# A graph layer's edge network: first layer as eight 32-row products, placed later in the step, and ten more one-hot picks

## The chip, the cores and the metric

The kernel runs on one core of one Trainium2 chip. The metric is the device time of one execution in microseconds; the median of 14 runs of the kernel before is 2398.38 us (2378.84 to 2437.09). A core has a matrix engine (TensorE, in the profile PE for its products and PEld for its weight loads), a vector engine (VectorE, DVE), a scalar engine (ScalarE, ACT), GpSimd (POOL) and a queue engine (SyncE, SP). Products land in PSUM, which has eight banks of 512 fp32 columns in each of 128 partitions.

## The reference, cut to what matters

N = 6250 nodes with F = 64 features, E = 200000 edges sorted by their target node, D = 32 edge attributes, M = 9 edge components, H = 64 hidden units.

```
w     = silu(edge_attr_32 @ W1 + b1) @ W2 + b2          # E x 9: 32 -> 64 -> 9, for every edge
h_src = x[src]                                          # E x 64: a gather of rows
msg   = einsum('ef,em,fmg->eg', h_src, edge_attr_9 * w, W_tp)
agg   = segment_sum(msg, dst, N) / 4
gamma, beta = split(silu(node_vec[:, None] @ Wn1 + bn1) @ Wn2 + bn2)
out   = layernorm(x + agg * (1 + gamma) + beta)
```

All of it is fp32. The change is in the first layer of `w` (32 to 64) and in how rows of `h_src` are fetched.

## The kernel before

**Blocks.** The edges are cut into tiles of 128 and the tiles into 98 blocks (`NBLK`) of 16 (`KB`). A loop over `i` does one step for each block, and a step works on several blocks at once: `i`, `i + 1`, `i + 2`, and for the gathers `i + 6` (`AHEAD`). The order of all instructions on each engine is that of the program text: `tc.manual_schedule()` leaves it as it is written, and only waits on semaphores are added.

**Two ways to fetch rows of x.** Of a block's 16 tiles, most are fetched by `gather` (L97): one indirect DMA for each tile, issued by GpSimd (L99). The last `picked(g)` tiles of a block, four or three, are "picked" instead: TensorE multiplies a one-hot matrix with a copy of x that lies in SBUF. One `pick` (L540) is 14 products of 128x128 with 448 columns (L552) into the PSUM tile `px` (two buffers), and then two VectorE instructions, `xm` (L561) and a reduction into `hs` (L563). The one-hot matrices come from `hots` (L533, L537), which read the key rows that ScalarE has copied into the PSUM tile `pk` in `keys` (L528, L531). `picked` (L52) gives three picks to every sixth block, in all 376 picks. In every fourth block from 7 on, one more row tile is fetched by single-row DMAs on SP (`load_rows`, L107), spread over four steps.

**The edge network.** `hidden(g)` (L476) is the first layer. The attributes of a block lie as 4 x 32 partitions by 512 columns, four groups of edges under one another. `w1bd` holds W1 four times in a block-diagonal pattern with zero blocks, 64 rows by 128 columns twice. So there are two products, each with 64 rows, 128 columns and 512 moving columns (L481), which TensorE carries out as two instructions each, and which fill the two banks of the PSUM tile `p1`. `hidden_act` (L488) is one SiLU over 128x1024 (L490) into `st[g]`. `second(g)` (L494, L499) is the second layer, from `st` into the PSUM tile `p2`, whose bank (tag `s`) it shares with `nodes`. ScalarE adds the bias (L502), and `weights` (L504) makes the matrix `a[g]` on VectorE (L509, L513, L519).

**Edge sums.** `windows(g)` (L571) multiplies the fetched rows `hs[g]` with `a[g]`: 16 products of 64 columns (L585) into the PSUM tiles `pz` (two buffers, each of 252 columns in a bank of 512), copied out by eight ScalarE copies (L596) into `z`. When these products are done, the buffer of `hs[g]` is free, and GpSimd may begin the gathers of block `g + 7`: there are seven buffers.

**A step** does, in this order: issue of gathers and loads; `keys(i + 2)`; `pick(i + 1, 0)` with the node work of `nodes(i)` between its products (L673, L648, L663 and, on VectorE, L402, L403 which read the bank `s`); `hots(i + 2)`; `hidden(i + 2)`; `second(i + 1)`; `windows(i)`; in odd steps `project(i // 2)` (L618, L632, then a transpose L638 whose results ScalarE and VectorE read in `halves`, L606 and L607; its PSUM tile has the tag `p1` too); `pick(i + 1, 1)` with `weights(i + 1)`; and `pick(i + 1, 2)`, `pick(i + 1, 3)`. The middle of the step reads:

```
                if i + 2 < NBLK:
                    hidden(i + 2)
                if i == NBLK - 2:
                    break
                second(i + 1)
                windows(i)
                turn = project(i // 2) if i % 2 == 1 else []
```

All eight PSUM banks are in use: `p1` two, `pz` two, `px` two, `s` and `r` one each.

Of the kernel before, what the change touches and what calls it, by code (L numbers as in the profile page):

```python
# [7 lines left out]
F32 = mybir.dt.float32  # L8
# [4 lines left out]
AF = mybir.ActivationFunctionType  # L13
# [15 lines left out]
LB = 2  # L29
Q = 4  # L30
J = 7
SPS = 4
SPG = range(7, NBLK, SPS)
# [17 lines left out]

def picked(g):  # L52

    return Q - (g % 6 == 0 and g < NBLK - LB)


def tiles(g):
# [10 lines left out]
def gnn_resnorm_kernel(ctx: ExitStack, tc: tile.TileContext, x, src, dst, dst_row, ea, sh, cn,  # L68
                       w1, b1, w2, b2, wtp, wn1, bn1, wn2, bn2, out):
    nc = tc.nc  # L70
# [6 lines left out]
    w1bd = consts.tile([P, 2 * H], F32)  # L77
    b1c = even(consts, P, 1, F32, name="b1c")
# [8 lines left out]
    with ExitStack() as fast:  # L87
        loads = fast.enter_context(tc.tile_pool(name="loads", bufs=3))
        work = fast.enter_context(tc.tile_pool(name="work", bufs=2))
        gath = fast.enter_context(tc.tile_pool(name="gath", bufs=AHEAD + 1))  # L90
        keep = fast.enter_context(tc.tile_pool(name="keep", bufs=1))
        psum = fast.enter_context(tc.tile_pool(name="psum", bufs=1, space=bass.MemoryType.PSUM))
        late = fast.enter_context(tc.tile_pool(name="late", bufs=2))

        hs, hs_dma = {}, {}

# [22 lines left out]
        w2p = keep.tile([P, D], F32)  # L119
# [50 lines left out]
                lambda: nc.vector.scalar_tensor_tensor(jl[:, c0:c1], kh, -float(J) / P, rest,  # L170
                                                       op0=ALU.mult, op1=ALU.add)]

        def keys_turn(g0, kf, tag, kt):

            c0 = g0 * Q
            p_kt = psum.tile([P, P], F32, tag=tag, name=f"p_kt{g0}", bufs=1 + (tag == "pz"))
            nc.tensor.transpose(p_kt, kf, ident)
            nc.scalar.copy(kt, p_kt)
            return lambda: nc.sync.dma_start(kd[c0:c0 + P, :], kt)
# [9 lines left out]
        KC = P // Q  # L189
        KN = 10 * KB  # L190

        def setup(temp):
# [19 lines left out]
            for c in range(KB // 4):  # L212
                q = c * D
# [44 lines left out]
            one = temp.tile([1, 1], F32)  # L258
            nc.vector.memset(one, 0.0)

            def keys_first(g, kf, tag):

                pk_t[g] = psum.tile([P, Q, P], F32, tag=tag, name=f"pk{g}", bufs=1 + (tag == "pz"))
                spread = []
                for t in range(picked(g)):
                    c = (g + 1) * Q - picked(g) + t
                    d0 = NBLK * KB + c * P
                    dg = xb.rearrange("p j f -> p (j f)")[:, d0:d0 + P]
                    nc.vector.tensor_scalar(dg, ident, kf[:, c:c + 1], None, op0=ALU.mult)
                    spread.append(lambda t=t, dg=dg: nc.tensor.matmul(pk_t[g][:, t, :], ones, dg,  # L270
                                                                      start=True, stop=True))
                return spread
# [6 lines left out]
            kb = [ztw[:, k * LB * Q:(k + 1) * LB * Q] for k in range(6)]  # L279
            for f in keys_of(0, LB, kb):  # L280
                f()
            for f in keys_first(0, kb[0], "pz"):
                f()
            spread = keys_first(1, kb[0], "r")
            pw_i = temp.tile([P, 1], I32)
            nc.vector.tensor_scalar(pw_i, pf, 147.0, None, op0=ALU.mult)
            nc.vector.tensor_scalar(pw_i, pw_i, 10, None, op0=ALU.logical_shift_right)
# [22 lines left out]
            pick(0, 2)  # L310
            hidden(1, act=False)
            kt = temp.tile([P, P], F16)
            keys_turn(LB, kb[0], "pz", kt)()
            hidden_act(1)
            load_keys(LB)
            p_row = psum.tile([len(SPG), P], F32, tag="pz", name="p_row", bufs=2)
# [6 lines left out]
            p_f = psum.tile([KB, NBLK], F32, tag="pz", name="p_f", bufs=2)  # L323
            nc.tensor.matmul(p_f, first_t, ident[0:NBLK, 0:NBLK], start=True, stop=True)
            nc.scalar.copy(first_f, p_f)
            p_cn = psum.tile([P, NJ], F32, tag="pz", name="p_cn", bufs=2)
# [16 lines left out]
            hots(1, 2, 3)  # L343
            pick(1, 1)
            nc.vector.tensor_copy(lo, lo_i)
            p_nid = psum.tile([P, NBLK], F32, tag="pz", name="p_nid", bufs=2)
# [129 lines left out]
        def hidden(g, act=True):  # L476

            e = ea_t.pop(g)
            p1 = psum.tile([P, 2, KB * P // 4], F32, tag="p1", name=f"p1_{g}")
            for i in range(2):  # L480
                nc.tensor.matmul(p1[:, i, :].rearrange("p (c t e) -> p c t e", c=4, t=4), w1bd[i * 64:(i + 1) * 64, :],  # L481
                                 e[i * 64:(i + 1) * 64, :].rearrange("p (t c e) -> p c t e", t=4, c=4),
                                 start=True, stop=True)
            p1_t[g] = p1
            if act:
                hidden_act(g)

        def hidden_act(g):  # L488
            st[g] = work.tile([P, 2, KB * P // 4], F32, tag="st", name=f"st{g}")
            nc.scalar.activation(st[g], p1_t.pop(g), AF.Silu, bias=b1c)  # L490

        p2, p2s = {}, {}

        def second(g):  # L494

            s = st.pop(g)
            p2[g] = psum.tile([P, 2, 2 * P], F32, tag="s", name=f"p2_{g}")
            for c in range(KB // 4):
                nc.tensor.matmul(p2[g][c * D:(c + 1) * D, 0, :].rearrange("p (i e) -> p i e", i=2), w2p,  # L499
                                 s[:, :, c * P:(c + 1) * P], start=True, stop=True)  # L500
            p2s[g] = work.tile([P, 2 * P], F32, tag="p2s", name=f"p2s{g}")
            nc.scalar.activation(p2s[g], p2[g][:, 0, :], AF.Identity, bias=b2c)  # L502

        def weights(g):  # L504

            p, v = p2.pop(g), p2s.pop(g)

            def part():
                nc.vector.transpose(p[:, 1, :], v)  # L509
                sw = p[:, 0, 0:KB * M].rearrange("p (t m) -> p t m", m=M)  # L510
                sh = sh_t.pop(g)
                for i in range(2):
                    nc.vector.tensor_mul(  # L513
                        sw[:, 8 * i:8 * i + 8].rearrange("p (s c) m -> p s c m", s=2),
                        p[:, 1, i * P:(i + 1) * P].rearrange("p (c q) -> p c q", q=D)[:, :, 0:2 * M]
                        .rearrange("p c (s m) -> p s c m", s=2),
                        sh[:, 8 * i:8 * i + 8].rearrange("p (s c) m -> p s c m", s=2))
# [53 lines left out]
        def windows(g, k0s=None):  # L571

            nk = tiles(g)
            end = g == NBLK - 1
            hsg, ag = hs[g], a[g]
            z = zs[g] if g in zs else sums(g)


            for k0 in range(0, nk, ZT) if k0s is None else k0s:
                n = min(ZT, nk - k0)  # L580
                pz = [psum.tile([P, ZT // 2, M, W], F32, tag="pz", name=f"pz{g}_{k0}", bufs=2)]
                pz.append(psum.tile([P, ZT // 2, M, W], F32, tag="px", name=f"pz{g}_{k0}_", bufs=2) if end else pz[0])
                for k in range(n):
                    v = k % 2
                    mm = nc.tensor.matmul(pz[v][v * F:(v + 1) * F, k // 2].rearrange("p m w -> p (m w)"),  # L585
                                          hsg[:, k0 + k, :], ag[:, k0 + k].rearrange("p m w -> p (m w)"),
                                          start=True, stop=True)
                    if k0 + k == 0:

                        for d in hs_dma.pop(g)[(g not in SPG):]:  # L590
                            tc.add_manual_dep(mm.ins, d.ins.name, mybir.DependencyInfo(
                                mybir.DependencyClass.Sync, mybir.DependencyReason.DATA), reason="rows of the group")
                for v in range(2):
                    copy = nc.vector.tensor_copy if end and k0 == ZT and v == 1 else nc.scalar.copy
                    for h in range(2):
                        copy(  # L596
                            z[h * F:(h + 1) * F, 0:5 - h, k0 + v:k0 + n:2, :].rearrange("p m k w -> p k m w"),
                            pz[v][v * F:(v + 1) * F, 0:(n + 1 - v) // 2, h:M:2, :])
# [91 lines left out]
        with tc.manual_schedule(), tc.tile_pool(name="temp", bufs=1) as temp:  # L690
# [6 lines left out]
            for i in range(1, NBLK):  # L697
# [22 lines left out]
                    hots(i + 2, 2, Q)  # L720
                if 56 <= i <= 58:
                    reach(i - 56)
                if i + 2 < NBLK:
                    hidden(i + 2)
                if i == NBLK - 2:
                    break
                second(i + 1)
# [9 lines left out]
                for t in range(2, Q + 1):  # L737
                    for f in beside[(t - 2) * n:(t - 1) * n]:
                        f()
                    if t < Q:  # L740
                        pick(i + 1, t)
                    if t == 2 and ends:
                        ends.pop(0)()
                if i in (3, 5):
                    tables.append(keys_turn(LB + KC * (i - 1) // 2, kb[0], "s", kt))

            g = NBLK - 1
            q = NJ - 1
# [247 lines left out]
```

## Time and profile before

| | us |
|---|---|
| median of 14 runs | 2398.38 (2378.84 to 2437.09) |
| the profiled execution: its time | 2407.98 |
| its span from the first to the last instruction | 2406.2 |
| TensorE products busy (PE) | 1695.5, 70% |
| GpSimd busy (POOL) | 1102.3, 46% |
| VectorE busy (DVE) | 1212.3, 50% |
| ScalarE busy (ACT) | 519.6, 22% |
| granted clock of TensorE, mean | 0.835 |

How to read it: a line of a group or of the timeline gives the source line, the engine, the operation, what is written and from what (by the program's names; `p` stands for `p1_g` and for `p2_g`), the shape, and the count. In square brackets stands the idle time of the engine just before, and what ended it; "remote" is a release whose origin the profile can't tell. Matmul ends are modelled: a row tells when TensorE was given its product, and a semaphore that tells others of it may come later. The profiled execution is 9.60 us (0.4%) over the median of the runs.

### The profile page before, as it was taken

How to read it: one execution, taken by the hardware profiler on the slowest of the kernel's cores; microseconds unless marked ns; L12 is line 12 of the kernel's file. 1: busy time of each engine (PE TensorE's matmuls, PEld its weight loads, DVE VectorE, ACT ScalarE, POOL GpSimd, SP SyncE). 2: the span in 40 equal slices, each digit the busy share in tenths (PEclk: the TensorE clock that was granted, in tenths of full speed). 3: DMA queues.
4: the chain of work that ended last, by engine and by line, in shares of the span. 5: the costliest groups of instructions: out<-in, count | busy, mean ns of one | idle time of the engine just before them, and what ended most of it. 6: DMA issues, size and time to landing. Idle time of an engine off the chain costs nothing. (4 is left out here: it accounts for less than half of the span.)

```text
span 2406.2 us, 34396 instructions
## 1 busy us (share of the span) xinstructions
PE 1695.5 (70%) x10929; PEld 1368.6 (57%) x10929; DVE 1212.3 (50%) x2194; ACT 519.6 (22%) x1323; POOL 1102.3 (46%) x1173
## 2 busy tenths in 40 slices
PE   3167677777676868778777766676776676767698
PEld 2056465656565656556665655565655555655587
DVE  2055454555454545545455545444554454544476
ACT  1021121222121212212122222121212122212132
POOL 7634444445354454454544545344535445445410
PEclk6578788888888889888888888788888888878799
DMA  3121111211111112111111211111111111111110
GB/s 117 23 63 51 36 32 37 51 34 38 50 35 35 33 37 52 34 37 45 42 34 34 51 33 36 45 35 33 35 47 37 31 32 35 49 35 34 33 38 5
DMA packets 90153, 95.99 MB, mean 40 GB/s; under 512 B 36697, under 2 KB 51243, under 8 KB 89963
## 3 DMA queue, kind: packets, MB, share of 16 engines
q0 software_dynamic: 37248, 38.22, 8.4%
q1 hardware_dynamic: 52138, 53.89, 7.4%
q8 instruction: 89, 1.46, 0.3%
q10 hardware_dynamic: 576, 1.61, 0.2%
q14 instruction: 102, 0.83, 0.1%
HBM read 91.88 MB, written 1.73 MB: 39 GB/s over the span
## 5 line engine op out<-in xcount | busy, mean ns | idle before, releaser
L552 PE MATMUL px<-xs_w,hot_k 128*128 128x448 f32 x5264 | 1317.3, 405 | 535.3 <-DVE xm L561 430.2
L99 POOL DMA_INDIRECT hs<-in_x_dram,src_i x1164 | 1101.0, 946 | 1196.3 <-PE pz L585 867.1
L552 PEld LDWEIGHTS px<-xs_w,hot_k 128*128 128x128 f32 x5264 | 1074.7, 212 | 670.0 <-DVE xm L561 462.7
L561 DVE SCALAR_TENSOR_TENSOR xm<-li,jl,px 128x448 f32<-128x448 f32 x376 | 254.6, 677 | 1022.8 <-remote 715.2
L537 DVE TENSOR_TENSOR hot_k<-pk,nk 128x896 fp32r<-128x896 f32 x376 | 391.9, 1081 | 0.6 <-ACT pk L531 0.6
L490 ACT ACTIVATE st<-p,b1c 128x1024 f32<-128x1024 f32 x98 | 109.2, 1115 | 881.0 <-PE p L481 710.4
L563 DVE TENSOR_REDUCE hs<-xm 128x64 f32<-128x448 f32 x376 | 233.1, 620 | 13.0
L596 ACT COPY ztw<-pz 64x140 f32<-64x140 f32 (+1 forms) x780 | 209.2, 268 | 29.7 <-PE pz L585 15.3
L585 PEld LDWEIGHTS pz<-a,hs 128*64 128x64 f32 x3116 | 117.0, 157 | 54.4 <-issue 50.4
L481 PE MATMUL p<-ea,w1bd 64*128 64x512 f32 x392 | 128.4, 652 | 22.2 <-issue 21.8
L499 PE MATMUL p<-st,w2p 128*32 128x256 f32 x784 | 75.3, 445 | 86.6 <-DVE xb L403 53.1
L585 PE MATMUL pz<-a,hs 128*64 128x63 f32 x3116 | 131.9, 246 | 5.1 <-issue 3.1
L519 DVE TENSOR_TENSOR a<-oh,p 128x1008 f32<-128x1008 f32 x98 | 118.0, 1204 | 3.3
L499 PEld LDWEIGHTS p<-st,w2p 128*32 128x32 f32 x784 | 17.7, 114 | 167.0 <-issue 105.8
L654 ACT COPY carry<-ps 128x128 f32<-128x128 f32 x48 | 12.7, 266 | 421.1 <-PE ps L648 359.4
L607 DVE TENSOR_TENSOR r<-pt,r 112x128 fp32r<-112x128 f32 x48 | 14.0, 291 | 120.3 <-issue 106.2
L481 PEld LDWEIGHTS p<-ea,w1bd 64*128 64x128 f32 x392 | 34.1, 189 | 62.8 <-issue 59.9
L502 ACT ACTIVATE p2s<-p,b2c 128x256 f32<-128x256 f32 x98 | 46.0, 469 | 100.5 <-remote 69.5
L632 PE MATMUL pt<-ztw,wtc 128*64 128x112 f32 x960 | 63.4, 285 | 0.0
L531 ACT CAST pk<-kr 128x512 f32<-128x512 f16 (+1 forms) x96 | 54.7, 570 | 18.1 <-DVE hot_k L537 15.2
L632 PEld LDWEIGHTS pt<-ztw,wtc 128*64 128x64 f32 x960 | 55.8, 158 | 0.1
L606 ACT CAST r<-pt 112x128 fp32r<-112x128 f32 x48 | 12.8, 266 | 176.1 <-PE px L552 101.0
(158 smaller groups left out, 557.8 us busy)
## 6 DMA issues: line engine op xcount, KB each, us to landing
hs<-in_x_dram SPq DMA_DIRECT2D x2944, 0.2 KB
ea<-in_ea_dram SPq DMA_DIRECT2D x48, 512.0 KB
hs<-in_x_dram,src_i POOLq DMA_INDIRECT x1164
kr<-kd SPq DMA_DIRECT2D x48, 256.0 KB
sh<-in_sh_dram SPq DMA_DIRECT2D x49, 144.0 KB
cb<-cn_d SPq DMA_DIRECT2D x12, 128.0 KB
out_dram<-o SPq DMA_DIRECT2D x23, 64.0 KB
dst_i<-in_dst_dram SPq DMA_DIRECT2D x1, 768.0 KB
```

The costliest lines, as they stand in the source:

```text
L99: hs_dma[g] = [nc.gpsimd.indirect_dma_start(out=hs[g][:, t - g * KB, :], out_offset=None, in_=x, in_offset=bass.IndirectOffsetOnAxis(ap=sr ...
L481: nc.tensor.matmul(p1[:, i, :].rearrange("p (c t e) -> p c t e", c=4, t=4), w1bd[i * 64:(i + 1) * 64, :], e[i * 64:(i + 1) * 64, :].rearra ...
L490: nc.scalar.activation(st[g], p1_t.pop(g), AF.Silu, bias=b1c)
L499: nc.tensor.matmul(p2[g][c * D:(c + 1) * D, 0, :].rearrange("p (i e) -> p i e", i=2), w2p, s[:, :, c * P:(c + 1) * P], start=True, stop=True)
L519: nc.vector.tensor_mul(a[g], oh_t.pop(g)[:, :, None, :].to_broadcast([P, KB, M, W]), sw.unsqueeze(3).to_broadcast([P, KB, M, W]))
L537: nc.vector.tensor_tensor(hot_k[g, t], pk_t[g][:, t, None, :].to_broadcast([P, J, P]), nk.unsqueeze(2).to_broadcast([P, J, P]), op=ALU.is_ ...
L552: nc.tensor.matmul(px.rearrange("p f l -> p (f l)"), hot_k[g, t][:, h, :], xs[i][:, h].rearrange("p f l -> p (f l)"), start=(h == 0 and i ...
L561: nc.vector.scalar_tensor_tensor(xm, li[:, None, :].to_broadcast([P, F, J]), jl[:, c:c + 1], px, op0=ALU.is_equal, op1=ALU.mult)
L563: nc.vector.tensor_reduce(hs[g][:, tiles(g) - q + t, :], xm, AX.X, ALU.add)
L585: mm = nc.tensor.matmul(pz[v][v * F:(v + 1) * F, k // 2].rearrange("p m w -> p (m w)"), hsg[:, k0 + k, :], ag[:, k0 + k].rearrange("p m w ...
L596: copy(z[h * F:(h + 1) * F, 0:5 - h, k0 + v:k0 + n:2, :].rearrange("p m k w -> p k m w"), pz[v][v * F:(v + 1) * F, 0:(n + 1 - v) // 2, h:M ...
L632: nc.tensor.matmul(pt[h * F:(h + 1) * F, 0, 0:KW], wtc2[:, c, :], z[h][:, c], start=(c == 0), stop=(c == 4))
```

## The change

Three edits go together.

1. `hidden` is cut into eight products of 32 rows, 64 columns and 256 moving columns, one for each of the four row groups and each half of its edges, without the zero blocks of `w1bd`. Row groups 0 and 1 write the lower 256 columns of the two banks of `p1`; row groups 2 and 3 write the upper 256 columns of the two banks of `pz`, which becomes one tile `pzw` that lives through the whole kernel. The SiLU becomes two instructions, one for each of the two tiles.
2. `hidden(i + 2)` is no longer called between `pick(i + 1, 0)` and `second(i + 1)`, but after `pick(i + 1, 2)`, that is after `windows(i)` and before `pick(i + 1, 3)`.
3. `picked` gives three picks to every sixteenth block instead of every sixth: 386 picks instead of 376, and ten gathers fewer. Fourteen blocks go from three picks to four, four blocks (16, 32, 64, 80) from four to three.

The order of the columns of `st` changes with it, and `second` and `weights` read and write in the new order with as many instructions of the same sizes. In `setup`, what used `pz` now uses parts of `pzw`.

```
 def picked(g):
-    return Q - (g % 6 == 0 and g < NBLK - LB)
+    return Q - (g % 16 == 0 and g < NBLK - LB)
...
+        pzw = psum.tile([P, 2, 4 * P], F32, tag="pz", name="pzw")
...
             e = ea_t.pop(g)
-            p1 = psum.tile([P, 2, KB * P // 4], F32, tag="p1", name=f"p1_{g}")
-            for i in range(2):
-                nc.tensor.matmul(p1[:, i, :].rearrange("p (c t e) -> p c t e", c=4, t=4), w1bd[i * 64:(i + 1) * 64, :],
-                                 e[i * 64:(i + 1) * 64, :].rearrange("p (t c e) -> p c t e", t=4, c=4),
-                                 start=True, stop=True)
-            p1_t[g] = p1
+            p1 = psum.tile([P, 2, 4 * P], F32, tag="p1", name=f"p1_{g}")
+            p1_t[g] = [p1[:, :, 0:2 * P], pzw[:, :, 2 * P:]]
+            for s in range(2):
+                for q in range(4):
+                    nc.tensor.matmul(p1_t[g][q // 2][s * H:(s + 1) * H, q % 2].rearrange("p (c t e) -> p c t e", c=4, t=2),
+                                     w1bd[q * D:(q + 1) * D, (q % 2) * H:(q % 2 + 1) * H],
+                                     e[q * D:(q + 1) * D].rearrange("p (s t c e) -> p s c t e", s=2, t=2, c=4)[:, s],
+                                     start=True, stop=True)
...
-            st[g] = work.tile([P, 2, KB * P // 4], F32, tag="st", name=f"st{g}")
-            nc.scalar.activation(st[g], p1_t.pop(g), AF.Silu, bias=b1c)
+            st[g] = work.tile([P, 4, 2 * P], F32, tag="st", name=f"st{g}")
+            for i, p1 in enumerate(p1_t.pop(g)):
+                nc.scalar.activation(st[g][:, 2 * i:2 * i + 2], p1, AF.Silu, bias=b1c)
...
-                pz = [psum.tile([P, ZT // 2, M, W], F32, tag="pz", name=f"pz{g}_{k0}", bufs=2)]
+                pz = [pzw[:, k0 // ZT, 0:ZT // 2 * M * W].rearrange("p (k m w) -> p k m w", m=M, w=W)]
...
-                if i + 2 < NBLK:
-                    hidden(i + 2)
                 if i == NBLK - 2:
                     break
                 second(i + 1)
...
                     if t < Q:
                         pick(i + 1, t)
+                    if t == 2 and i + 2 < NBLK:
+                        hidden(i + 2)
```

In the built programs the order and the waits are then these.

- TensorE: the eight products come between the last product of `pick(i + 1, 2)` and the first of `pick(i + 1, 3)`. In odd steps they wait for VectorE (L607 has read `pt`, the last user of `p1`), in even steps for the last of ScalarE's copies out of `pzw`.
- TensorE, in `windows`: the products of a block's second eight tiles wait for ScalarE's fourth copy of the first eight tiles of the same block. The two halves lie in different banks, but in one tile, `pzw`. Before, each half had a tile of its own and waited, where it waited, for copies of the block before.
- ScalarE: the two SiLU instructions stand ahead of the next step's key copy into `pk` and of its copy of `carry` (L654), which stood ahead of them before. `second(i + 1)` waits for the second of them, which is now issued half a step ahead of it instead of a whole one.

More of the change, by code (lines that the diff above doesn't have):

```diff
@@ L171, in keys_of, with keys_turn @@
                                                        op0=ALU.mult, op1=ALU.add)]
-        def keys_turn(g0, kf, tag, kt):
+        def keys_turn(g0, kf, kt, p_kt=None):
             c0 = g0 * Q
-            p_kt = psum.tile([P, P], F32, tag=tag, name=f"p_kt{g0}", bufs=1 + (tag == "pz"))
+            if p_kt is None:
+                p_kt = psum.tile([P, P], F32, tag="s", name=f"p_kt{g0}")
             nc.tensor.transpose(p_kt, kf, ident)
@@ L259, in setup, with keys_first @@
             nc.vector.memset(one, 0.0)
-            def keys_first(g, kf, tag):
-                pk_t[g] = psum.tile([P, Q, P], F32, tag=tag, name=f"pk{g}", bufs=1 + (tag == "pz"))
+            def keys_first(g, kf, pk):
+                pk_t[g] = pk
                 spread = []
@@ L281, in setup @@
                 f()
-            for f in keys_first(0, kb[0], "pz"):
+            for f in keys_first(0, kb[0], pzw[:, 0].rearrange("p (t e) -> p t e", t=Q)):
                 f()
-            spread = keys_first(1, kb[0], "r")
+            spread = keys_first(1, kb[0], psum.tile([P, Q, P], F32, tag="r", name="pk1"))
             pw_i = temp.tile([P, 1], I32)
@@ L312, in setup @@
             kt = temp.tile([P, P], F16)
-            keys_turn(LB, kb[0], "pz", kt)()
+            keys_turn(LB, kb[0], kt, pzw[:, 1, 0:P])()
             hidden_act(1)
             load_keys(LB)
-            p_row = psum.tile([len(SPG), P], F32, tag="pz", name="p_row", bufs=2)
+            p_row = pzw[0:len(SPG), 0, 0:P]
             nc.tensor.transpose(p_row, row_f, ident)
@@ L322, in setup @@
             near(0)
-            p_f = psum.tile([KB, NBLK], F32, tag="pz", name="p_f", bufs=2)
+            p_f = pzw[0:KB, 1, 0:NBLK]
             nc.tensor.matmul(p_f, first_t, ident[0:NBLK, 0:NBLK], start=True, stop=True)
             nc.scalar.copy(first_f, p_f)
-            p_cn = psum.tile([P, NJ], F32, tag="pz", name="p_cn", bufs=2)
+            p_cn = pzw[:, 0, 0:NJ]
             nc.tensor.matmul(p_cn, cn_j, ident[0:NJ, 0:NJ], start=True, stop=True)
@@ L345, in setup @@
             nc.vector.tensor_copy(lo, lo_i)
-            p_nid = psum.tile([P, NBLK], F32, tag="pz", name="p_nid", bufs=2)
+            p_nid = pzw[:, 1, 0:NBLK]
             nc.tensor.matmul(p_nid, sel[0:KB], first_f, start=True, stop=True)
@@ L498, in second @@
             for c in range(KB // 4):
-                nc.tensor.matmul(p2[g][c * D:(c + 1) * D, 0, :].rearrange("p (i e) -> p i e", i=2), w2p,
-                                 s[:, :, c * P:(c + 1) * P], start=True, stop=True)
+                nc.tensor.matmul(p2[g][c * D:(c + 1) * D, 0, :].rearrange("p (q e) -> p q e", q=4), w2p,
+                                 s[:, :, c * 2 * D:(c + 1) * 2 * D], start=True, stop=True)
             p2s[g] = work.tile([P, 2 * P], F32, tag="p2s", name=f"p2s{g}")
@@ L513, in part @@
                     nc.vector.tensor_mul(
[L514 to L517, printed above, removed]
+                        sw.rearrange("p (q s t) m -> p q s t m", s=2, t=2)[:, :, i],
+                        p[:, 1, :].rearrange("p (q t d) -> p q t d", q=4, t=2)[:, :, :, i * M:(i + 1) * M],
+                        sh.rearrange("p (q s t) m -> p q s t m", s=2, t=2)[:, :, i])
                 a[g] = work.tile([P, KB, M, W], F32, tag="a", name=f"a{g}")
@@ L744, in gnn_resnorm_kernel @@
                 if i in (3, 5):
-                    tables.append(keys_turn(LB + KC * (i - 1) // 2, kb[0], "s", kt))
+                    tables.append(keys_turn(LB + KC * (i - 1) // 2, kb[0], kt))
             g = NBLK - 1
```

## The prediction

> **What bounds the kernel now.** I read the page first: no engine is busy for more than 70%, and the list of groups has GpSimd waiting for the edge sums.
>
> ```profile
> PE 1695.5 (70%) x10929; PEld 1368.6 (57%) x10929; DVE 1212.3 (50%) x2194; ACT 519.6 (22%) x1323; POOL 1102.3 (46%) x1173
> ...
> L99 POOL DMA_INDIRECT hs<-in_x_dram,src_i x1164 | 1101.0, 946 | 1196.3 <-PE pz L585 867.1
> ...
> L596 ACT COPY ztw<-pz 64x140 f32<-64x140 f32 (+1 forms) x780 | 209.2, 268 | 29.7 <-PE pz L585 15.3
> ```
>
> GpSimd's idle time before the gathers, 867.1 us, ends with the last product of `windows` (L585). So steps form a ring: end of `windows`, 0.28 us, then 11 to 13 gathers of 0.94 + 0.30 us each, then the rest of TensorE's step up to the next `windows`. Next the timeline, of a step after an odd `windows`:
>
> ```profile
> 1601.02 0.94 POOL L99 DMA_INDIRECT hs<-in_x_dram,src_i  x1 [0.30 <-issue]
> 1603.12 0.68 DVE L561 SCALAR_TENSOR_TENSOR xm<-li,jl,px 128x448 f32<-128x448 f32 x1 [7.28 <-remote]
> ...
> 1603.86 5.11 PE L552 MATMUL px<-xs_w,hot_k 128*128 128x448 f32 x16 [9.99 <-DVE xm L561]
> 1604.67 0.68 DVE L561 SCALAR_TENSOR_TENSOR xm<-li,jl,px 128x448 f32<-128x448 f32 x1 [0.21 <-remote]
> ...
> 1611.55 1.13 PE L481 MATMUL p<-ea,w1bd 64*128 64x512 f32 x4
> ...
> 1612.61 0.64 PE L499 MATMUL p<-st,w2p 128*32 128x256 f32 x8
> ...
> 1613.18 1.15 PE L585 MATMUL pz<-a,hs 128*64 128x63 f32 x32
> ...
> 1614.10 1.97 ACT L596 COPY ztw<-pz 64x140 f32<-64x140 f32 x7
> ...
> 1614.62 0.95 POOL L99 DMA_INDIRECT hs<-in_x_dram,src_i  x1 [12.65 <-PE pz L585]
> ```
>
> While gathers run, signals from TensorE reach the other engines late: `xm` waited 7.28 us for a pick whose products had been given to TensorE long before, and TensorE then stood 9.99 us for a free `px`. All arrear has come some 2.5 us after the last gather's end (1601.96 to 1604.67 here); I call this the flush. After it come pick 3, the next pick 0, the first layer, the second and `windows`, with no gap. A step after an even `windows`:
>
> ```profile
> 1291.05 1.13 PE L481 MATMUL p<-ea,w1bd 64*128 64x512 f32 x4
> 1292.01 0.94 POOL L99 DMA_INDIRECT hs<-in_x_dram,src_i  x1 [0.30 <-issue]
> 1295.29 0.68 DVE L561 SCALAR_TENSOR_TENSOR xm<-li,jl,px 128x448 f32<-128x448 f32 x1 [7.25 <-remote]
> ...
> 1297.03 1.08 PE L499 MATMUL p<-st,w2p 128*32 128x256 f32 x8 [4.85 <-DVE xb L403]
> 1298.04 1.98 PE L585 MATMUL pz<-a,hs 128*64 128x63 f32 x32
> ```
>
> Here the first layer is done before the flush and costs nothing. Taking each block's first L585 as a mark, the 89 steps from 179.88 to 2306.70 us are 45 even ones of 21.48 us mean and 44 odd ones of 26.37. Without gathers (2306.70 to 2381) a step takes 14.1 to 15.5 us and TensorE has no gap.
>
> **Part 1: `hidden` moves behind pick 2.** In each of the 89 steps the timeline shows what stood before `second`. In 58 it starts as `hidden` ends, and both pick 0 and L403 were done about 1.0 us earlier: gain 0.99 each, 57.8 us. In 4 a part is gained, 1.8; in 27, mostly even ones like the one above, nothing. What hides it at its new place is TensorE's wait for the flush: 9.99 us above, and 4.85 us of slack in the other step. L606 always came by 8.7 us after the first gather, so the new wait for L607 ends before the flush; the queue behind it is pick 3, which waits for a later VectorE instruction anyway. If that cover fails, it costs 1.13 again. Sum: -59.6.
>
> **Part 2: eight narrow products.** L481 shows two products side by side, four instructions in 1.13 us; half the columns with four row groups side by side give 0.57 at best. It matters only in the five gatherless steps: -2.5, between 0 and -2.8. "TensorE: Matmul & The Clock Gate", Part 3 on packing, states 3.07 times for four row tiles of 512 columns; no row here has four row groups, and by it this term would be about -3.
>
> **Part 3: the new wait in `windows`.** The products of the second eight tiles now wait for four copies of the first eight. Before, TensorE went from one half to the next with no gap: 32 instructions in 1.15 us, while the copies ran on behind. In all 97 full blocks the first four copies take 1.10 us (from the timeline; rows of 281 and 256 ns, two each). Ahead of them: products still draining at the end of the first half, 0.11, and 0.05 until ScalarE starts, as where it was idle (0.23 where the bias copy and the SiLU were in its way, and the SiLU is gone from there). Behind them 0.06, as from the end of `xm` at 1603.80 to the product at 1603.86. Sum 1.32. Nothing covers it: behind the waiting product stand `project`, picks 1 to 3 and `hidden` on TensorE, and GpSimd's next gathers wait for the last product, so the ring is longer by all of it; in the gatherless steps TensorE is the bound. 1.3 x 97 = +126, between 1.1 (copies alone) and 1.5 (bias copy always in the way): 107 to 146.
>
> The page "PSUM — Partial Sum Buffer", section on bank collisions, asks for guards by bank and quadrant. No run here shows a collision. By it the halves, in two banks, would need no wait; the sum would be 126 lower, about -43. The program waits by tile, and the built order decides.
>
> **Part 4: two SiLUs, half a step before their use.** Nearest rows: 587 ns (128x512 cast, L531) and 815 ns (64x512 SiLU, L398), so 1.17 to 1.63 us for two instead of 1.115. After a flush they run beside `xm`, its reduction, L402 and L403 (0.68 + 0.62 + 0.34 = 1.64), for which `second` waits anyway. In the 20 even steps that end right after the flush this costs 0 to 0.3: +4 (0 to 12, if the first SiLU starts late). The key copy (0.59) and `carry` behind them are due 5 us after the flush in odd steps (1609.64): 0.
>
> **Part 5: ten more picks.** Odd steps with three picks (and 13 gathers) take 25.08 us on average (15 of them), with four picks and 12 gathers 27.03 (29): +1.95 for ten, +19.5. But `hidden` was in the way in all steps with four and in 8 of 15 with three, so -4.7 comes back: +14.9. Bounds: a pick before the flush costs nothing and the gather is saved, -12.5; a pick wholly after it is 14 products at 5.11/16 us less 1.25, 3.2 each, +32.
>
> **The sum.** 126 - 59.6 - 2.5 + 4 + 14.9 = +83. On the profiled execution (2407.98, 9.60 over the median of the runs) that gives 2491; on the median, 2398.4 + 83 = 2481.
>
> **Rivals.**
>
> *No net change (2409).* The wait is paid only in part, because TensorE's time after `windows` is slack in even steps (4.85 us above). For it: that slack. Against it: the gathers start from the same last product, and the flush moves with them. With the wait on the path only in the 58 steps and 5 more where TensorE runs through, 63 x 1.3 = 82 and the sum is +39, 2437; for no change it would also need the least price of the picks, -12.5, giving +11.
>
> *Faster (2378).* TensorE's signals get through during the gathers. They did in 16 of the 29 odd four-pick steps (first `xm` under 13.5 us after the first gather; 25.8 us a step) and not in 13 (28.6). If every pick's signal comes before the flush, the 13 late steps gain 2.8 each (36), the 25 even steps that now run on after the flush become like the other 20 (22.2 to 20.6, 39), and an added pick is free (14.9 to -12.5, 27): 83 - 102 = -19. For it: the load before the flush changes. Against it: fewer gathers by only ten in 1164, and the signal of pick 1 stands ahead of everything moved. It decides if the first `xm` of odd steps comes under 13.5 us in nearly all.
>
> *Much slower (2545).* `hidden`'s products crawl among the gathers, as they did in seven steps where TensorE got them over 12 us after the first gather (3.4 to 5.2 us), and push pick 3 and pick 0 of the 20 short even steps behind the flush: 3.2 each, +64. Against it: products under 9 us ran at full speed.
>
> **How the numbers follow.** About 0.5% (12 us) can be told from no change here. Forecast 0.72, at 2481, own range 2440 to 2520; no net change 0.10, of which 0.05 within 12 us and 0.05 slower; faster 0.07; much slower 0.11. Faster 0.07, same 0.05, slower 0.88. The bounds of all terms give +26 to +144. I leave out the faster rival and most of the much slower one: 2425 to 2525.
>
> **What would show it.** In the profile after: in every step a gap of about 1.3 us between products 16 and 32 of `windows`, ended by the copy on ScalarE; `windows` about 2.4 us instead of 1.15; the first layer between picks 2 and 3, done before the flush; `second` right behind pick 0; odd steps about 27.2 us, even ones 22.4. The prediction is wrong if that gap is missing or GpSimd starts before the second half ends; if the first layer still ends after the flush; or if odd steps fall under 26.

## The result, and the profile after

The changed kernel takes 2579.62 us (median of ten runs, 2561.62 to 2583.76), the kernel before 2399.3 beside it: the ratio is 1.077, 95% interval 1.074 to 1.080. It is taken from the fast runs of each kernel alone, while the median of the kernel before is over all its 47 runs, slower ones among them. The forecast was 2481 in a range up to 2525. So the direction was right, and the loss is 180 us instead of 83.

The page of the changed kernel (2558.4 us of span, granted clock 0.822), in groups as before: busy time, mean ns of one, idle time ahead and what ended most of it.

```profile
PE 1822.7 (71%) x12245; PEld 1402.0 (55%) x12245; DVE 1246.1 (49%) x2224; ACT 551.6 (22%) x1423; POOL 1097.6 (43%) x1163
...
L100 POOL DMA_INDIRECT hs<-in_x_dram,src_i x1154 | 1096.3, 950 | 1344.1 <-PE pzw L589 1018.3
L556 PE MATMUL px<-xs_w,hot_k 128*128 128x448 f32 x5404 | 1430.4, 412 | 307.3 <-issue 192.4
...
L589 PE MATMUL pzw<-a,hs 128*64 128x63 f32 x3116 | 142.4, 237 | 143.6 <-ACT ztw L600 120.1
...
L485 PE MATMUL pzw<-ea,w1bd 32*64 32x256 f32 x784 | 114.6, 418 | 65.6 <-issue 62.9
```

The same two groups in the page of the kernel before:

```profile
L552 PE MATMUL px<-xs_w,hot_k 128*128 128x448 f32 x5264 | 1317.3, 405 | 535.3 <-DVE xm L561 430.2
...
L585 PE MATMUL pz<-a,hs 128*64 128x63 f32 x3116 | 131.9, 246 | 5.1 <-issue 3.1
```

Two things are new. `windows` (L589) now waits for ScalarE's copy, 120.1 us in all, which was forecast. And the idle time before the picks (L556) is no longer ended mainly by `xm`, as 430.2 of the 535.3 us before, but by "issue" (192.4 of 307.3): TensorE waited for nothing that the profile shows, and still gave out no product. This was not forecast. The timeline of a step after an even `windows` shows both; it is the counterpart of the short step from 1291.05 on that the prediction shows:

```profile
1263.78 0.94 POOL L100 DMA_INDIRECT hs<-in_x_dram,src_i  x1 [9.60 <-PE pzw L589]
...
1269.25 0.43 PE L485 MATMUL p<-ea,w1bd 32*64 32x256 f32 x2
...
1269.87 3.07 PE L556 MATMUL px<-xs_w,hot_k 128*128 128x448 f32 x14
...
1274.55 0.67 PE L556 MATMUL px<-xs_w,hot_k 128*128 128x448 f32 x2 [1.61 <-DVE xm L565]
...
1276.65 0.56 PE L677 MATMUL ps<-wn2a,ht 65*128 65x128 f32 x1 [1.15 <-issue]
...
1278.06 0.53 PE L556 MATMUL px<-xs_w,hot_k 128*128 128x448 f32 x1 [0.84 <-issue]
...
1279.46 4.03 PE L556 MATMUL px<-xs_w,hot_k 128*128 128x448 f32 x11 [0.87 <-issue]
...
1279.56 0.69 ACT L495 ACTIVATE st<-p,b1c 128x512 f32<-128x512 f32 x1 [14.90 <-remote]
1279.76 0.68 DVE L565 SCALAR_TENSOR_TENSOR xm<-li,jl,px 128x448 f32<-128x448 f32 x1 [4.61 <-remote]
1280.15 0.68 ACT L495 ACTIVATE st<-pzw,b1c 128x512 f32<-128x512 f32 x1
...
1283.42 0.64 PE L504 MATMUL p<-st,w2p 128*32 128x256 f32 x8
1283.99 0.69 PE L589 MATMUL pzw<-a,hs 128*64 128x63 f32 x16
...
1285.88 0.68 PE L589 MATMUL pzw<-a,hs 128*64 128x63 f32 x16 [1.20 <-ACT ztw L600]
```

The flush is at 1279.6. The first layer ran at 1269.25 in 0.62 us and pick 3 right behind it; but of the next pick 0, which began at 1274.55, only three products went out in almost five microseconds, two at once and one 3.5 us later, and eleven were left for after the flush. In its counterpart in the kernel before, pick 0 and the first layer behind it were done by then.

Two counts from the traces make this a number, over the 91 runs of at least eight gathers (one in each of 90 steps, and a first one ahead of the steps), and the 89 steps between the marks of `windows` that the prediction used. I call a *stall* a pause of over 0.55 us from the start of one product to that of the next, where the second waits for no semaphore, from the first gather to 3.5 us behind the last. The second count is that of pick products which TensorE starts later than 2.2 us behind the last gather, that is after the flush.

| | steps with stalls, of 91 | pick products after the flush, even / odd steps | step, even / odd, us |
|---|---|---|---|
| before | 16 | 4.9 / 15.4 | 21.48 / 26.37 |
| forecast for the change | | | 22.4 / 27.2 |
| changed | 90 | 10.5 / 18.2 | 24.14 / 26.88 |

The odd steps came as forecast (0.3 below). The 45 even ones take 1.74 us more than forecast, 78 us in all.

### The profile page after: what moved, and what is told of

Read it like the earlier page. It is cut to its first block, busy times and chain, and to the rows that moved or that the text cites. A ratio compares the mean times of both kernels' runs of the same rounds, so it can differ in the third digit from the quotient of the medians.

```text
span 2558.4 us, 37137 instructions
## 1 busy us (share of the span) xinstructions
PE 1822.7 (71%) x12245; PEld 1402.0 (55%) x12245; DVE 1246.1 (49%) x2224; ACT 551.6 (22%) x1423; POOL 1097.6 (43%) x1163
## 4 chain that ended last, share of the span: by engine, by line
PE 48%; another core or an unknown queue 18%; issue 16%; DVE 13%; ACT 5%; DMA 0%; DVEq 0%; ACTq 0%
PE px L556 36%; PE pzw L589 4%; DVE xm L565 4%; DVE hot_k L541 3%; ACT ztw L600 3%; PE p L504 2%; PE pt L636 2%; DVE hs L567 2%; DVE a L523 1%; PE p L485 1%; PE ps L677 1%; PE pzw L485 1%; PE ps L667 1%; DVE p L518 1%
## 5 line engine op out<-in xcount | busy, mean ns | idle before, releaser
L100 POOL DMA_INDIRECT hs<-in_x_dram,src_i x1154 | 1096.3, 950 | 1344.1 <-PE pzw L589 1018.3
L556 PE MATMUL px<-xs_w,hot_k 128*128 128x448 f32 x5404 | 1430.4, 412 | 307.3 <-issue 192.4
L556 PEld LDWEIGHTS px<-xs_w,hot_k 128*128 128x128 f32 x5404 | 1117.3, 215 | 542.9 <-issue 280.5
L495 ACT ACTIVATE st<-p,b1c 128x512 f32<-128x512 f32 x98 | 67.3, 687 | 1131.5 <-remote 1047.9
L589 PE MATMUL pzw<-a,hs 128*64 128x63 f32 x3116 | 142.4, 237 | 143.6 <-ACT ztw L600 120.1
L600 ACT COPY ztw<-pzw 64x140 f32<-64x140 f32 (+1 forms) x780 | 208.9, 268 | 132.8 <-PE pzw L589 110.7
L589 PEld LDWEIGHTS pzw<-a,hs 128*64 128x64 f32 x3116 | 114.6, 146 | 206.4 <-ACT ztw L600 134.0
L485 PE MATMUL pzw<-ea,w1bd 32*64 32x256 f32 x784 | 114.6, 418 | 65.6 <-issue 62.9
L485 PE MATMUL p<-ea,w1bd 32*64 32x256 f32 x784 | 68.4, 402 | 34.0 <-issue 27.1
L485 PEld LDWEIGHTS pzw<-ea,w1bd 32*64 32x64 f32 x784 | 34.3, 133 | 90.9 <-issue 90.9
L495 ACT ACTIVATE st<-pzw,b1c 128x512 f32<-128x512 f32 x98 | 66.6, 680 | 0.0
```

The lines of the kernel that those rows point to most:

```text
L100: hs_dma[g] = [nc.gpsimd.indirect_dma_start(out=hs[g][:, t - g * KB, :], out_offset=None, in_=x, in_offset=bass.IndirectOffsetOnAxis(ap=sr ...
L485: nc.tensor.matmul(p1_t[g][q // 2][s * H:(s + 1) * H, q % 2].rearrange("p (c t e) -> p c t e", c=4, t=2), w1bd[q * D:(q + 1) * D, (q % 2) ...
L495: nc.scalar.activation(st[g][:, 2 * i:2 * i + 2], p1, AF.Silu, bias=b1c)
L556: nc.tensor.matmul(px.rearrange("p f l -> p (f l)"), hot_k[g, t][:, h, :], xs[i][:, h].rearrange("p f l -> p (f l)"), start=(h == 0 and i ...
L600: copy(z[h * F:(h + 1) * F, 0:5 - h, k0 + v:k0 + n:2, :].rearrange("p m k w -> p k m w"), pz[v][v * F:(v + 1) * F, 0:(n + 1 - v) // 2, h:M ...
```

## Experiments

All ratios are to the kernel before, run beside the experiment on the same chip, with 95% intervals. One thing is needed to understand the first four numbers: when they were taken, the kernel before took 1486 us instead of 2399, and for all later ones 2406 to 2408.

### Four parts alone, where no signal is late

The edits: `e1_split` makes the two banks two tiles, `e3_move_only` moves the wide first layer in the kernel before, `e4_picks` changes the picks alone, `e7_split_picks` is `e1_split` with the old picks.

```
 # e1_split, on the changed kernel
-        pzw = psum.tile([P, 2, 4 * P], F32, tag="pz", name="pzw")
+        pzw = [psum.tile([P, 4 * P], F32, tag=f"pz{k}", name=f"pzw{k}") for k in range(2)]
...
 # e3_move_only, on the kernel before
-                if i + 2 < NBLK:
-                    hidden(i + 2)
                 if i == NBLK - 2:
...
+                    if t == 2 and i + 2 < NBLK:
+                        hidden(i + 2)
```

> The changed kernel with the edge sums' two banks as two tiles, so that the second half of `windows` waits for no copy of the first; the first layer's upper halves then need three SiLUs instead of two. Theory W (the wait is the largest term, and it lies on the ring): the gap inside `windows` goes, 120 us of it as L589's idle time shows, and three SiLUs give 0 to 10 back: 2580 - 120 = 2460, 2445 to 2475. Rival C (the ring is set by TensorE's instructions that go out one at a time among the gathers, and the gap inside `windows` is mostly covered by that): 2520 to 2575, with L556's idle time on issue larger than 192 us.

> The kernel before with one edit: `hidden`, in its two wide products, behind pick 2. No new wait, no narrow products, no more picks. Theory W, the prediction's own working: 58 steps gain 0.99 each, 2399 - 58 = 2341, 2330 to 2365. Rival C: what stands behind `hidden` on TensorE, pick 3 and the next pick 0, is pushed later among the gathers and goes out one product at a time; the gain is used up: 2385 to 2440, with more idle time on issue before L552 than in the kernel before.

> The kernel before with one edit: one block of 16 instead of one of 6 has three picks, 386 picks for 376. The prediction's working: +14.9 (from -12.5 to +32), less what `hidden` in its old place adds again, up to +19.5: 2399 + 17 = 2416, 2387 to 2431. Under rival C ten picks cost the same.

> As the kernel with two tiles, and with the picks of the kernel before (376): what is left of the change is the eight narrow products, three SiLUs and the later place. Theory W: 2399 - 60 - 2 + 4 to 10 = 2345, 2330 to 2365. Rival C: 2420 to 2470, more than the move of the two wide products alone if the number of TensorE's instructions in the stretch of the gathers decides (64 with weight loads instead of 8), the same as that if only the place decides.

Measured: 0.999 (0.998 to 1.000), 1.010 (1.009 to 1.012), 1.005 (1.003 to 1.006) and 1.001 (1.000 to 1.002), at 1484 to 1500 us. None of my expectations was made for that, and the page says why. The row of `xm` and that of the gathers, first from this run of `e4_picks`, then from the same kernel measured later, at 2420 us (its page, too):

```profile
L99 POOL DMA_INDIRECT hs<-in_x_dram,src_i x1154 | 1091.8, 946 | 353.5 <-issue 320.5
...
L561 DVE SCALAR_TENSOR_TENSOR xm<-li,jl,px 128x448 f32<-128x448 f32 x386 | 260.8, 676 | 202.5 <-PE px L552 199.9
```

```profile
L99 POOL DMA_INDIRECT hs<-in_x_dram,src_i x1154 | 1092.3, 947 | 1209.0 <-PE pz L585 883.2
...
L561 DVE SCALAR_TENSOR_TENSOR xm<-li,jl,px 128x448 f32<-128x448 f32 x386 | 261.1, 676 | 1004.1 <-remote 734.6
```

The gathers and `xm` last equally long in both, and all of the difference is idle time. In the first trace half of the `xm` start within 0.04 us of their pick's last product, and nine of ten within 0.94; in the second the same two figures are 4.4 and 11.5 us. So the late signals of the prediction's first section are a condition that the chip was in and not a property of the program. Without it TensorE is busy for 98% of the span and neither stalls nor waits to speak of. It is not one specimen of the chip either: on one and the same chip the kernel before took 1485.64 us beside these four and 2407.83, some nine minutes later, beside the next ones. What brings it on, no run shows. The four had to be measured again where signals are late, as in the result.

### The same again, the change itself, and the wait alone, where signals are late

`e1b_split` and `e3b_move_only` are the kernels above. `e8_wait_only` is the kernel before with the two `pz` as one tile:

```
+        pzw = psum.tile([P, 2, 4 * P], F32, tag="pz", name="pzw")
...
-                pz = [psum.tile([P, ZT // 2, M, W], F32, tag="pz", name=f"pz{g}_{k0}", bufs=2)]
+                pz = [pzw[:, k0 // ZT, 0:ZT // 2 * M * W].rearrange("p (k m w) -> p k m w", m=M, w=W)]
```

> The changed kernel as it is, beside the kernel before on one chip, since the kernel before took 1486 us on the chip of the first experiments and 2399 on that of the result. If the chip is like the first one of the experiments (TensorE busy for 98% of the span, granted clock 0.99): theory W says that nothing covers the gap inside `windows`, 97 x 1.2 = 116 of it, and the rest of the change is worth nothing there (the split kernel measured 0.999): 1486 + 116 = 1602, 1590 to 1620. Rival C has no say there, since no signal comes late. If the chip is like that of the result: 2580 again.

> The kernel before with one edit: the edge sums' two banks are one tile, as in the changed kernel, so that the second half of `windows` waits for the four copies of the first. First layer, its place and the picks are those of before. Theory W: the gap alone costs 97 x 1.2 to 1.3 = 116 to 126: 1602 to 1612 where the kernel before takes 1486, 2515 to 2525 where it takes 2399. Rival C (where signals come late the gap is covered by the ring's own slack): under 2460 there, and the same as theory W where they do not.

> The changed kernel with the two banks as two tiles, a second time, for a chip on which signals from TensorE come late. There theory W: 2460, 2445 to 2475; rival C: 2520 to 2575. On a chip like that of the first experiments: 0.999 of before again.

> The kernel before with `hidden` behind pick 2 and nothing else, a second time, for a chip on which signals from TensorE come late. There theory W: 2341, 2330 to 2365; rival C: 2385 to 2440. On a chip like that of the first experiments: 1.010 of before again.

Measured, beside 2407.83: the change 2569.33, 1.072 (1.064 to 1.080); the wait alone 2526.46, 1.056 (1.047 to 1.065); the change without the wait 2492.93, 1.039 (1.031 to 1.047); the move alone 2327.89, 0.972 (0.965 to 0.979). The wait is worth its +119 alone, as theory W says; its row in `e8_wait_only`:

```profile
L587 PE MATMUL pzw<-a,hs 128*64 128x63 f32 x3116 | 154.3, 250 | 137.5 <-ACT ztw L598 134.0
```

In the whole change it is worth only 2569 - 2493 = 76. And the move, which rival C took for the culprit, is a gain of 80. Neither theory holds as it stands: 2493 is 85 over the kernel before with the wait gone and a gain of 80 in it, so 165 us lie in what is left, the narrow products, their SiLUs and the ten picks.

### Which of these it is

`e7b_split_picks` takes the picks out of the 165. The next two start from the move alone. `e11_cut_columns` cuts each wide product into four of 128 columns: the instructions are then as many as for the narrow ones. `e12_two_signals` gives each wide product a tile and a SiLU of its own: one signal more.

```
 # e11_cut_columns
-            for i in range(2):
-                nc.tensor.matmul(p1[:, i, :].rearrange("p (c t e) -> p c t e", c=4, t=4), w1bd[i * 64:(i + 1) * 64, :],
-                                 e[i * 64:(i + 1) * 64, :].rearrange("p (t c e) -> p c t e", t=4, c=4),
+            for c in range(4):
+                for i in range(2):
+                    nc.tensor.matmul(p1[:, i, c * P:(c + 1) * P].rearrange("p (t e) -> p t e", t=4), w1bd[i * 64:(i + 1) * 64, :],
+                                     e[i * 64:(i + 1) * 64, :].rearrange("p (t c e) -> p c t e", t=4, c=4)[:, c],
...
 # e12_two_signals
-            p1 = psum.tile([P, 2, KB * P // 4], F32, tag="p1", name=f"p1_{g}")
+            p1 = [psum.tile([P, 4 * P], F32, tag=f"p1{i}", name=f"p1_{g}_{i}") for i in range(2)]
...
+            for i, p1 in enumerate(p1_t.pop(g)):
+                nc.scalar.activation(st[g][:, i, :], p1, AF.Silu, bias=b1c)
```

> Eight narrow products behind pick 2, two tiles, the picks of the kernel before, where signals come late (the kernel before near 2400). Known there by now: the wait alone +119, the move of the two wide products alone -80, the changed kernel without the wait +85. So narrow products, SiLUs and picks together cost 165 on top of the move. Theory N (TensorE gives out about 60 products from the first gather on at full speed, and after that one in 0.7 us or a multiple; narrow products use 16 of the 60 instead of 4): nearly all of the 165 is theirs: 2460 to 2485. Rival P (the ten picks are dear): 2340 to 2380. Where no signal is late: 1.001 of before again.

> The kernel before with `hidden` behind pick 2, and its two wide products of 512 columns each cut into four of 128 columns: 16 product rows and 16 weight loads in the trace as for the narrow ones, but the row groups, the two banks, the one SiLU and the one signal of the kernel before. Theory N (the number of TensorE's instructions among the gathers): products stall from about the 55th after the first gather in nearly every step, 2440 to 2490. Rival S (what costs is the second signal to ScalarE, or four row groups at a time): as the move alone, 2320 to 2350, with stalls in 30 steps at most. Where no signal is late: 1.010 of before, and up to 0.02 more for the weight loads.

> The kernel before with `hidden` behind pick 2 in its two wide products, each in a tile and with a SiLU of its own: two signals from TensorE to ScalarE instead of one, four product rows as before. Rival S (signals that wait for delivery hold TensorE up): stalls in most steps, 2400 or more. Theory N: as the move alone, 2320 to 2345.

> The kernel before with 386 picks instead of 376, where signals come late. The prediction's working: +15 to +20, 2415 to 2430. Theory N: about the same, since each of the ten steps gets 14 more products and one gather less. Rival P: 2480 or more. Where no signal is late: 1.005 of before again.

Measured, beside 2406.3 (the first row is that of above, beside 2407.83):

| | us | ratio | steps with stalls | pick products after the flush, even / odd | step, even / odd |
|---|---|---|---|---|---|
| the move alone (`e3b_move_only`) | 2327.89 | 0.972 | 26 | 1.3 / 13.3 | 20.39 / 25.49 |
| `e12_two_signals` | 2339.52 | 0.971 (0.959 to 0.984) | 26 | 2.4 / 14.2 | 20.55 / 25.92 |
| `e11_cut_columns` | 2483.43 | 1.037 (1.027 to 1.048) | 91 | 11.0 / 20.9 | 22.86 / 26.67 |
| `e7b_split_picks` | 2494.31 | 1.042 (1.032 to 1.052) | 91 | 11.2 / 21.2 | 22.84 / 26.72 |
| `e4b_picks` | 2420.34 | 1.012 (1.001 to 1.022) | 8 | 4.6 / 19.6 | 21.18 / 26.90 |

`e4b_picks` gives +14, about the prediction's price, in an interval from some +2 to +54: rival P's 2480 falls. A second signal costs nothing that can be told, and `e11_cut_columns` stalls without four row groups: rival S falls. The wide first layer, merely cut into more instructions, loses 156 us against the move alone, nearly as much as the narrow one's 166. Theory N stands: it is the number of TensorE's instructions among the gathers. Weight loads, of which there are as many, are held like products: in the changed kernel's steps there are 533 such pauses between the starts of two instructions, loads counted too, 252 before a load and 281 before a product, and 375 of them are of 0.65 to 0.75 us. Nor do stalls come from waiting for instructions to be fetched: a transfer of instructions (the pages' DMA queues q8 and q14) was under way in only 33 of the changed kernel's 402 stalls, and in 12 of 362 in the steps of `e11_cut_columns`. The rows of the first layer and of the picks, of the move alone and then of `e11_cut_columns`:

```profile
L552 PE MATMUL px<-xs_w,hot_k 128*128 128x448 f32 x5264 | 1299.4, 398 | 313.8 <-DVE xm L561 232.8
...
L481 PE MATMUL p<-ea,w1bd 64*128 64x512 f32 x392 | 115.2, 654 | 25.0 <-issue 25.0
```

```profile
L553 PE MATMUL px<-xs_w,hot_k 128*128 128x448 f32 x5264 | 1396.6, 414 | 330.1 <-issue 197.1
...
L482 PE MATMUL p<-ea,w1bd 64*128 64x128 f32 x1568 | 164.1, 301 | 223.1 <-issue 215.5
```

And a step after an even `windows` with eleven gathers in each timeline. First the move alone:

```profile
1245.59 1.98 PE L585 MATMUL pz<-a,hs 128*64 128x63 f32 x32
...
1247.49 5.88 PE L552 MATMUL px<-xs_w,hot_k 128*128 128x448 f32 x28
...
1253.30 1.13 PE L481 MATMUL p<-ea,w1bd 64*128 64x512 f32 x4
...
1254.36 3.56 PE L552 MATMUL px<-xs_w,hot_k 128*128 128x448 f32 x16
...
1257.90 2.71 PE L552 MATMUL px<-xs_w,hot_k 128*128 128x448 f32 x12
...
1263.66 0.68 DVE L561 SCALAR_TENSOR_TENSOR xm<-li,jl,px 128x448 f32<-128x448 f32 x1 [8.70 <-remote]
...
1265.40 1.08 PE L499 MATMUL p<-st,w2p 128*32 128x256 f32 x8 [4.79 <-DVE xb L403]
```

Then `e11_cut_columns`:

```profile
1229.41 1.15 PE L586 MATMUL pz<-a,hs 128*64 128x63 f32 x32
1230.49 5.87 PE L553 MATMUL px<-xs_w,hot_k 128*128 128x448 f32 x28
1236.29 1.16 PE L482 MATMUL p<-ea,w1bd 64*128 64x128 f32 x16
1237.38 3.58 PE L553 MATMUL px<-xs_w,hot_k 128*128 128x448 f32 x16
...
1243.79 0.46 PE L553 MATMUL px<-xs_w,hot_k 128*128 128x448 f32 x1
1245.89 0.53 PE L553 MATMUL px<-xs_w,hot_k 128*128 128x448 f32 x1 [1.64 <-issue]
1246.60 4.09 PE L553 MATMUL px<-xs_w,hot_k 128*128 128x448 f32 x10 [0.18 <-issue]
1250.62 1.08 PE L500 MATMUL p<-st,w2p 128*32 128x256 f32 x8
```

The first layer takes the same time in both, 1.1 us. With four instructions the last 12 products of pick 0 run at 1257.90, 10 to 13 us after the first gather (1247.85), and TensorE then stands 4.79 us for the flush: the slack that the prediction counted on. With 16 it stops at about 10 us after the first gather (1230.84), two products come singly, and ten run after the flush, right in front of `second`. There they are also dearer: the ten take 4.09 us at a granted clock of 0.50 (1246.60 to 1250.60), 0.41 each, while the twelve of the move alone took 0.23 each at 1.00. In all even steps of the changed kernel, pick products behind the flush come 0.39 us apart, at a mean clock of 0.53.

### Does it come from the place, does the rest add up, and is there a shorter kernel

```
 # e5b_narrow_old_place: e1_split with `hidden` back before `second`
 # e16_all_but_narrow: e8_wait_only with the move, the wide products, and % 16 in `picked`
 # e13_move_fewer_picks: e3_move_only with
-    return Q - (g % 6 == 0 and g < NBLK - LB)
+    return Q - (g % 2 == 0 and g < NBLK - LB)
```

> The changed kernel with two tiles, and `hidden` back between the next pick 0 and `second`, where no gather runs any more in most steps: narrow products in the old place. Its SiLUs read the edge sums' banks just ahead of `windows`, so `windows` has to wait for them: 0.69 + 2 x 0.45 us of SiLUs, less the 0.64 of `second`, some 0.9 x 97 = 90. Theory N (narrow products are dear only among the gathers): stalls in 30 steps at most, and 2407 + 14 + 90 = 2510, 2440 to 2530, without a stall to explain it. Rival D (they are dear wherever they stand): stalls in most steps, and 2570 or more.

> The changed kernel without the narrow products: two wide products behind pick 2 with one SiLU, one tile for both banks with its wait, 386 picks. Theory N: the sum of the parts measured alone, 2407 - 80 + 119 + 14 = 2460, 2425 to 2475, a little less if the later place covers a part of the wait; that is about what the prediction's sum said for the whole change. Rival D (the parts make each other worse: the wait, or the picks, bring on the stalls that the place alone did not): stalls in most steps and 2510 or more.

> A version that might beat both: the kernel before with the two wide products of `hidden` behind pick 2, and three picks instead of four in one block of two (instead of one of six): 31 picks fewer, 31 gathers more, all in odd steps. From the trace of before, odd steps with three picks took 1.95 us less than those with four: 2328 - 31 x 1.95 = 2268, 2255 to 2300. Rival G (a gather costs what it lengthens the run of gathers by, 1.25 each, once the first layer is out of the way): 2328 + 39 = 2367.

Measured, beside 2406.18. `e5b_narrow_old_place`: 2455.33, but its four runs spread from 2419.74 to 2485.71, too wide for an interval. Its trace tells more: 10 steps with stalls, fewer than the 16 before, and `windows` waits 54.1 us for SiLUs. So narrow products are not dear as such; their place is.

`e16_all_but_narrow`: 2502.13, 1.049 (1.039 to 1.059), with 23 steps with stalls. Rival D's stalls are not there, but the parts measured alone sum to 2460, 42 less (69 by the profiled executions), and theory N's range ended at 2475. The traces place most of it. From the end of the last gather to the next `windows`, even steps take 5.98 us before, 4.85 with the move alone, 5.14 with the wait alone, 5.78 with the picks alone, and 4.93 here. So the move and the wait each shorten this stretch, but together no more than the move does: added up they would leave 3.81, and 1.1 us in each of 45 steps is 50. A lower clock goes with such stands, in the move alone as well: where TensorE waits for the flush, as before 1265.40 in the timeline of the move alone, the granted clock behind it is 0.50 (1265.40 to 1267.60; 1.00 from 1247.50 to 1260.60), and `windows` took 1.98 us there instead of 1.15. The rest stays open.

`e13_move_fewer_picks`: 2301.86, 0.962 (0.956 to 0.969), the shortest of all; expected were 2255 to 2300, for 31 picks fewer where the edit takes out 32. Fourteen products fewer in 32 of the odd steps leave 7.3 pick products after the flush in an odd step instead of 13.3, and odd steps take 24.95 us instead of 25.49. Rival G's 2367 is out. It was not run where no signal is late; there the move alone lost 1%.

## Why the prediction was wrong in size

**What bounds the kernel**: right. The gathers still start from the last product of `windows` (1018.3 us of L100's idle time), and the flush still ends each run of gathers.

**Part 1, the move, -59.6: the step that failed.** For the two wide products it is right and even too small: -80, since in 39 of 45 even steps of the move alone at most three pick products are left for after the flush (21 before). In the change it is the other way round. The step priced the work at its new place by time alone, under the cover of the wait for the flush, and the rival that could have caught it was put aside because "products under 9 us ran at full speed". That held for the first layer in even steps, where its last product goes out at some 5.8 us (in odd ones at over 9 us in 24 of 45). But the place is ahead of pick 3 and pick 0, and the step did not ask how many instructions they and it make together; Part 2 counted those of the narrow products at nothing. Sixteen rows of the narrow products instead of four bring on stalls in nearly every step, at a median of 57 products after the first gather. What the runs put in place of -59.6 and -2.5: -80 for the move and +166 for the narrow products (with their SiLUs) in that place; `e11_cut_columns` loses 156 by the number of instructions alone, with wide rows. With the wait's 76 and nothing for the picks these give +162; the change measured beside them was +161.5 (2569.33 against 2407.83).

**Part 2, -2.5**: the eight products do run side by side, 0.62 us from their first (1269.25) to the next product (1269.87), where the two wide ones took 1.06 (1253.30 to 1254.36). The prediction's 0.57 was good; the rows that come with it were counted as free. "TensorE: Matmul & The Clock Gate", Part 3 on packing, gives 3.07 times for four row tiles of 512 columns. By that figure, 0.57 x 4 / 3.07 = 0.74 us and a term of about -2 is the estimate, and not the -3 that the prediction put. The trace agrees that packing speeds the array up, by 1.06 / 0.62 = 1.7 here, and the runs add a cost by the instruction that the section doesn't weigh.

**Part 3, +126**: the mechanism, the place and the size of the gap were right: 1.20 us, 120.1 in all, and +119 alone. In the whole change it costs 76: with and without it odd steps take 26.88 and 26.81 us, even ones 24.14 and 22.86. In odd steps the time from the last gather to the next `windows` falls from 10.50 to 9.11 us with the wait, and 18.2 pick products instead of 23.8 are left for after the flush, so the wait is taken back there; why only there is open. "PSUM — Partial Sum Buffer", section on bank collisions, asks for guards by bank and quadrant; `e1_split` agrees for the two halves, since two tiles in the same banks run without the wait.

**Part 4, +4**: two SiLUs ended 2.6 us before `second` in the step above (1280.83 against 1283.42): 0 there.

**Part 5, +14.9**: +14 alone; in the changed kernel nothing (2492.93 with ten more picks, 2494.31 without).

**The rivals.** "Much slower" (2545, 0.11) had the effect: pick 3 and pick 0 of even steps behind the flush. It was put too low and told by the wrong sign. I expected `hidden`'s own products to crawl, while most of the changed kernel's stalls, 242 of 402, stand before pick products and 78 before its own; I priced 20 even steps, while all 45 have four products or more after the flush, and I priced a product there at 5.11/16 = 0.32 us, while in even steps it took 0.39. "Faster" failed on its own condition: the signals came no earlier (the first `xm` under 13.5 us in 24 of 45 odd steps, by the same count in 27 before). "No net change" would have needed the wait in even steps to be slack; they paid it in full (24.14 - 22.86 = 1.28).

**The sum.** Of the 99 us between forecast and result, the profiled executions show 2560.2 - 2491 = 69: 78 from even steps, -14 from odd ones, and 5 elsewhere. The other 30 are the two executions: before's was 9.60 over its median, the changed one's 19.4 under. The bounds that the prediction gives for its terms add up to +32 to +130, not to +26 to +144; the measured +180 is outside of both. And none of its signs of being wrong came: the gap in `windows` is there, GpSimd waits for the second half, the first layer is given out before the flush in all 89 steps, and odd steps take 26.88. It had named no sign for even steps longer than 22.4, and there the loss lies.

## What to carry to other kernels

Work that is moved into another engine's shadow brings its instructions with it, not only its time: count them (some 50 to 60 products, each with its weight load, went out here) with everything that stands behind in the queue, and prefer few wide products there even if narrow ones are quicker. Two banks in one tile are one thing to wait for: two tiles, with a third SiLU, saved 76 us here. And a ratio holds for the condition it was taken in: a kernel whose time is set by late signals should be compared beside its predecessor, and where they are not late, too.

## What the runs showed of the hardware

- **TensorE's products among late signals.** While gathers run and signals come late, stalls set in after a number of products. With four rows of first layer, they set in after 59 to 63 products from the first gather (tenth to ninetieth percentile, the move alone), at 12.0 to 15.0 us; with 16 rows after 51 to 59, at 8.0 to 11.9 us (`e7b_split_picks`), and in every step. So time alone doesn't tell it: at 10 to 13 us the move alone ran at full speed. The pauses have a grain: of 402 in the changed kernel, 131 are of 0.6 to 0.8 us, 137 of 1.4 to 1.5 and 43 of 2.0 to 2.2. Loads and products are held alike; what it is that they fill, and what lets one out in 0.7 us, no run shows.
- **One program, two times.** `e4_picks` took 1492 us once and 2420 another time, with gathers of 946 and 947 ns and granted clocks of 0.998 and 0.838. The trace of the first holds 18017 landing signals of its 1154 gathers, that of the second 3146. Its cause stays open; the part of the change that cost most, the narrow products behind pick 2, costs nothing where signals are on time (`e7_split_picks`, 1.001).
